# Sums in PSUM at a register's column, and one gathered tile in sixteen copied on chip: a graph network layer on one core

## The chip, the cores and the metric

The kernel runs on one core of a Trainium2 chip. The core's engines are TensorE (PE, with its weight loads as PEld), VectorE (DVE), ScalarE (ACT), GpSimd (POOL) and SyncE (SP, which here only starts DMAs). Each works through its own list of instructions in order; they meet at semaphores. The metric is the device time of one launch in microseconds (us), the median of several runs.

## The reference

A graph of 12,500 nodes with 64 features and 200,000 edges with 32. The edges come sorted by destination `dst`; the sources `src` are random. Cut to what matters:

```
def _mlp(x, W1, b1, W2, b2):
    return jax.nn.relu(x @ W1 + b1) @ W2 + b2
msg_in = jnp.concatenate([nodes[row], nodes[col], edge_features], axis=-1)   # row = src, col = dst
messages = _mlp(msg_in, mW1, mb1, mW2, mb2)                                  # 160 -> 128 -> 64
aggregated = jax.ops.segment_sum(messages, col, num_segments=nodes.shape[0])
upd_in = jnp.concatenate([nodes, aggregated], axis=-1)
update = _mlp(upd_in, uW1, ub1, uW2, ub2)                                    # 128 -> 128 -> 64
out = _layernorm(x + update)
```

Destinations follow 12500 times the square of a uniform number, so that in the sorted list the first edges share few nodes and the last ones are spread over many.

## The kernel before

**Tiling.** 128 edges are a tile (1563 tiles, the last partly padding), 8 tiles a group `s` (SUB, 196 groups), 16 tiles a super-group `g` (SUP, 98). The first layer of the message network is split: `A = x @ mW1[:64]` for the sources, `B = x @ mW1[64:128] + mb1` for the destinations, and the edge's own part. Both tables are made in the kernel in chunks of 1024 nodes (`chunk_a`, `chunk_b`, L381 to L403) and written to DRAM.

**Sources.** `gather` (L147) starts one indirect DMA on GpSimd per tile (L158): 128 rows of the table, by the source numbers in `src_s`, into a row buffer `xg` of one group (ROWB = 6 buffers). While A is not ready, the first XG = 7 groups fetch rows of x instead (64 wide, two groups to a buffer) and TensorE transposes and multiplies them (`transpose`, L257).

**Destinations.** As the edges are sorted, the destinations of a tile lie within a window of 32 nodes from the tile's first one, `wint`. `windows` (L206) reads these window starts into registers of SyncE and copies 32 rows of B per tile into `rhs`, beside the edge weights. `select` (L176, VectorE) makes two one-hot selections, one inside `operand` (with the edge features, so that one matmul gives edge part plus B row) and one in `sel`; `counts` (L194, ScalarE) makes a bf16 copy of the latter.

**A step.** The main loop (L537) handles one group a step. `edge_part` (L243, TensorE, for the next group) puts the edge part and the B row into PSUM `pc`; `node_part` adds the gathered row (L263, VectorE) and applies the relu (L264, ScalarE); `collect` multiplies each tile's hidden layer by its selection (L276, 8 matmuls into `ph`, 32 columns each) and one matmul with `one0` gives the counts (L274); `aggregate` (L279, VectorE) loads the 8 window starts into registers and adds each tile's 32 columns of sums and counts into `comb` in SBUF at the column of its window (L288, 8 adds that follow one another).

**Node updates.** `comb` holds for all nodes the 128 summed hidden features, the counts, a row of ones and x transposed. An update handles 384 nodes (UB = 3 tiles). There are 54; `UPD` lists at which super-group each begins, every 2 to 15 super-groups in the first 62 and every single one from there. Each is spread over steps: `columns` (a copy of the x part, ScalarE, L297), `update` (L304, L305 on TensorE, relu on ScalarE), `residual` (L315, L316 and the statistics), `norm` (reciprocal, scaling, store by SyncE).

**What sets the order.** The order in each engine's list is the order of the program (a manual schedule); buffers that rotate make a later writer wait for the last reader. PSUM: `pc` two buffers of two banks, and one bank each for `pt`, `ph`, `pu` and `cps`. A fallback for inputs that break the window rule follows behind a flag and does not run here.

## Time and profile before

| | |
|---|---|
| median of 10 runs | 1990.76 us (1989.14 to 1994.73) |
| the profiled execution | 1991.83 us, its span 1990.0 us |
| busy, share of the span | PE 68%, PEld 60%, DVE 46%, ACT 18%, POOL 74% |
| granted TensorE clock, mean | 0.576 of full speed |
| DMA | 211.74 MB, 106 GB/s on the mean |
| instructions | DVE 2661, ACT 479, PE 7851, POOL 1572 |

The page cuts the span into 40 slices:

```
PE   3678976656566566666666666757767758577687
DVE  5347643534343444444444444445454545454544
POOL 7677777777777777777777777777777777777773
PEclk9965555555555555555556555565565665655655
```

A digit is the busy share in tenths (for PEclk the clock that the throttle granted). In the lists of groups, a line gives source line, engine, operation, output<-inputs and shapes, the number of instructions, then after the bar the busy time in us, the mean of one in ns, the idle time just before them and what ended it ("issue": the engine waited for nothing that the profile shows). A q behind an engine's name (DVEq, SPq) is its queue: register operations, waits and DMA starts, which are not counted as busy; their rows give shortest, median and longest in ns. TensorE's fp32 matmuls have two rows each.

### The profile page before, as it was taken

To read this page: it belongs to the slowest core of one execution; us is meant where nothing else is said; L and a number is where in the kernel's file an instruction comes from. 1 tells how busy PE (TensorE), PEld (TensorE's weight loads), DVE (VectorE), ACT (ScalarE), POOL (GpSimd) and SP (SyncE) were. 2 spreads that over 40 slices of the span, in tenths; PEclk is the share of its full clock that TensorE was granted. 3 is DMA by queue.
4 is the path that set the end of the run, shared out by engine and by line. 5 is a ranking of instruction groups with operands and counts; after the bars stand their busy time and mean duration, and the time that the engine had idled before them with its cause. 6 is when DMAs were issued, how large, how long until landed. Compare 5 with 4: busy or idle time off the path is not lost.

```text
span 1990.0 us, 31593 instructions
## 1 busy us (share of the span) xinstructions
PE 1351.1 (68%) x7851; PEld 1198.9 (60%) x7851; DVE 908.4 (46%) x2661; ACT 348.3 (18%) x479; POOL 1476.5 (74%) x1572
## 2 busy tenths in 40 slices
PE   3678976656566566666666666757767758577687
PEld 3577865656555565665655655647666647475666
DVE  5347643534343444444444444445454545454544
ACT  1121111111111111111111111121212112121211
POOL 7677777777777777777777777777777777777773
PEclk9965555555555555555556555565565665655655
DMA  8745554433333333333333333333333333333331
GB/s 219 219 118 151 159 139 117 115 88 100 87 100 89 100 90 100 91 91 98 99 91 99 92 100 91 98 96 97 98 96 100 97 99 97 100 95 101 95 99 43
DMA packets 244401, 211.74 MB, mean 106 GB/s; under 512 B 80542, under 2 KB 209022, under 8 KB 243824
## 3 DMA queue, kind: packets, MB, share of 16 engines
q0 software_dynamic: 50016, 100.70, 19.9%
q1 hardware_dynamic: 178644, 98.69, 17.9%
q10 hardware_dynamic: 15554, 10.31, 1.8%
q8 instruction: 63, 1.03, 0.2%
q14 instruction: 124, 1.02, 0.2%
HBM read 190.78 MB, written 18.68 MB: 105 GB/s over the span
## 4 chain that ended last, share of the span: by engine, by line
POOL 54%; issue 25%; DMA 8%; PE 8%; DVE 3%; SPq 1%; ACT 0%; ACTq 0%; DVEq 0%; POOLq 0%
POOL xg L158 54%; DMA xg<-tab_a,src_s 5%; PE ph L276 3%; DMA xl<-in_x1T 2%; PE pc L243 2%; DVE comb L288 1%; PE pu L304 1%; PE pb L381 1%; PE py L315 1%; DVE h L263 1%; PE pu L305 1%; PE py L316 0%; DMA rhs<-tab_b 0%; PE ph L274 0%; SPq L216 0%
## 5 line engine op out<-in xcount | busy, mean ns | idle before, releaser
L158 POOL DMA_INDIRECT xg<-tab_a,src_s x1507 | 1422.4, 944 | 468.7 <-issue 443.3
L276 PEld LDWEIGHTS ph<-sel,h 128*128 128x128 f32 x3126 | 601.6, 295 | 35.0 <-issue 35.0
L276 PE MATMUL ph<-sel,h 128*128 128x32 f32 x3126 | 593.1, 360 | 0.0
L263 DVE TENSOR_TENSOR h<-pc,xg 128x1024 f32<-128x1024 f32 (+1 forms) x190 | 230.8, 1215 | 774.9 <-DMA xg<-tab_a,src_s 712.8
L243 PE MATMUL pc<-rhs,l 64*128 64x128 f32 x3126 | 407.8, 413 | 69.7 <-DMA l<-in_eT 36.0
L288 DVE TENSOR_TENSOR comb<-comb,ph 128x64 f32 x1563 | 345.6, 221 | 201.8 <-ACT xw L297 82.0
L243 PEld LDWEIGHTS pc<-rhs,l 64*128 64x128 f32 x3126 | 352.8, 302 | 89.0 <-DVE rs L330 35.0
L264 ACT ACTIVATE h<-h 128x1024 f32<-128x1024 f32 (+1 forms) x190 | 199.2, 1049 | 919.2 <-DVE h L263 877.4
L304 PE MATMUL pu<-comb,w2u 128*128 x108 | 88.9, 927 | 260.6 <-DVE comb L288 260.6
L274 PE MATMUL ph<-selb,one 128*128 128x256 bf16 x196 | 74.4, 380 | 241.9 <-DVE comb L288 156.2
L304 PEld LDWEIGHTS pu<-comb,w2u 128*128 128x128 f32 x108 | 27.1, 311 | 276.0 <-DVE comb L288 276.0
L274 PEld LDWEIGHTS <-one 128*128 128x128 bf16 x196 | 26.6, 136 | 274.1 <-DVE comb L288 254.8
L185 DVE TENSOR_TENSOR l<-l,cps 128x1024 f32<-128x1024 int32 (+1 forms) x101 | 123.3, 1221 | 4.0 <-DMA rhs<-tab_b 0.5
L197 ACT CAST selb<-sel 128x512 bf16<-128x512 f32 x98 | 60.4, 616 | 326.3 <-DVE sel L189 298.9
L315 PE MATMUL py<-ux,xw 128*128 128x64 f32 x324 | 84.5, 353 | 0.7 <-ACT hTu L307 0.7
L316 PE MATMUL py<-u,hTu 128*128 128x64 f32 x324 | 81.7, 344 | 0.0
L305 PE MATMUL pu<-xw,uz 128*128 128x384 f32 x108 | 80.3, 847 | 0.0
L307 ACT ACTIVATE hTu<-pu,ub_s 128x384 f32<-128x384 f32 x54 | 31.4, 582 | 271.4 <-PE pu L305 271.4
L315 PEld LDWEIGHTS py<-ux,xw 128*128 128x128 f32 x324 | 66.6, 255 | 10.7 <-issue 5.6
L316 PEld LDWEIGHTS py<-u,hTu 128*128 128x128 f32 x324 | 67.9, 259 | 0.0
L189 DVE TENSOR_TENSOR sel<-cps,drc 128x512 f32<-128x512 f32 x98 | 66.9, 682 | 0.1
L158 POOL DMA_INDIRECT xg<-in_x,src_s x56 | 53.0, 947 | 18.7 <-issue 16.2
(73 smaller groups left out, 419.1 us busy)
## 6 DMA issues: line engine op xcount, KB each, us to landing
l<-in_dst_row SPq DMA_DIRECT2D x196, 128.0 KB
l<-in_eT SPq DMA_DIRECT2D x196, 128.0 KB
rhs<-tab_b SPq DMA_DIRECT2D x1563, 16.0 KB
xg<-tab_a,src_s POOLq DMA_INDIRECT x1507
tab_b<-tb SPq DMA_DIRECT2D x13, 512.0 KB
tab_a<-tb ACTq DMA_DIRECT2D x12, 512.0 KB
out<-o SPq DMA_DIRECT2D x54, 96.0 KB
comb<-in_x1T SPq DMA_DIRECT2D x6, 520.0 KB
```

Of the source, the lines that this page charges most:

```text
L158: nc.gpsimd.indirect_dma_start(out=a[:, i, :], out_offset=None, in_=A[:, :] if s >= XG else x[:, :], in_offset=bass.IndirectOffsetOnAxis(a ...
L185: nc.vector.tensor_tensor(l[r], l[r].bitcast(I32), node[r].unsqueeze(2).broadcast_to([r.stop - r.start, SUP // 2, P]), op=ALU.is_equal)
L243: nc.tensor.matmul(pc[:, b, k, :], L[g][q:q + 64, m, :], rhs[g % 2][q:q + 64, m, :], start=s >= XG or k == 0, stop=s >= XG)
L263: nc.vector.tensor_tensor(h[:, b, m], pc[:, b, m], a[:, b, m], op=ALU.add)
L264: nc.scalar.activation(h[:, b, m], h[:, b, m], AF.Relu)
L274: nc.tensor.matmul(ph[:, :n, 1, :], one0, SB[g][:, k0:k0 + n, :], start=True, stop=True)
L276: nc.tensor.matmul(ph[:, i, 0, :], h[:, i % 2, i // 2, :], S[g][:, k0 + i, :], start=True, stop=True)
L288: nc.vector.tensor_tensor(to, to, ph[:, i], op=ALU.add)
L304: nc.tensor.matmul(pu, w2u, comb[:, 0, bass.ds(n0, UB * P)], start=True, stop=False)
L305: nc.tensor.matmul(pu, uz, xw, start=False, stop=True)
L315: nc.tensor.matmul(py[:, i], xw[:, i * P:(i + 1) * P], ux, start=True, stop=False)
L316: nc.tensor.matmul(py[:, i], hT[:, i * P:(i + 1) * P], u2, start=False, stop=True)
```

## The change

1. *Sums and counts add up in PSUM.* `aggregate` and `comb` go. The whole period of an update, up to 384 columns, has one PSUM bank for sums (`sums`, two buffers) and one for counts (`cnt`). `opened` starts them with a matmul of zeros; `collect` loads 8 column offsets (`woff`, worked out once by `offsets`) into registers of TensorE and each tile's matmul adds at its offset; counts are 8 matmuls with a single column of ones. `carry` adds the 32 columns of the last window to the next period; `close` copies the banks to SBUF (ScalarE). The x columns of an update come by DMA (`columns`), no longer from `comb`. `pu`, `py` and the set-up matmuls share the rotation of `pc`.
2. *One tile of each two groups is not gathered.* From group 13 on, the last tile of each odd full group (`copied`) gets its x columns, 64x1 each, from `xcol` (x transposed, in SBUF): 128 copies at a column from a register, spread over two steps, 36 of each 64 on ScalarE and 28 on VectorE (`copies`), into one of two `xo`. A further matmul with `w1a` in `edge_part` makes its row of A, and its relu reads PSUM alone.
3. *Row buffers and order.* ROWB 6 to 14, XG 7 to 8; the row buffer has the order of `pc`. `windows` is called for a group, two steps ahead, instead of for a super-group. `relative`, `windows` and the offsets stand later among the first chunks; the memsets of `comb` are gone. The store of a finished update moves to the end of its step.

```
-ROWB = 6
-XG = 7
+ROWB = 14
+XG = 8
+CG = 2
+CF = 6 * CG
+CA = 36
+UW = UB * P
+    def copied(s):
+        return s >= CF and s % CG == CG - 1 and len(tiles(s)) == SUB
...
-        for i, t in enumerate(tiles(s)):
+        for i, t in enumerate(tiles(s)[:SUB - copied(s)]):
             nc.gpsimd.indirect_dma_start(
...
+                c = copied(s) and i == n - 1
                 nc.tensor.matmul(pc[:, b, k, :], L[g][q:q + 64, m, :], rhs[g % 2][q:q + 64, m, :],
-                                 start=s >= XG or k == 0, stop=s >= XG)
+                                 start=s >= XG or k == 0, stop=s >= XG and not c)
+                if c:
+                    nc.tensor.matmul(pc[:, b, k, :], xo[s // CG % 2][q:q + 64], w1a[q:q + 64], start=False, stop=True)
...
-                    nc.scalar.activation(h[:, b, m], h[:, b, m], AF.Relu)
+                    nc.scalar.activation(hf[:, m], hf[:, m], AF.Relu)
+                if copied(s):
+                    nc.scalar.activation(h[:, 1, SUB // 2 - 1], pc[:, 1, SUB // 2 - 1], AF.Relu)
...
+        def opened(u):
+            ps = psum.tile([DH, UW], F32, name="sums")
+            pn = psum.tile([1, UW], F32, name="cnt", bufs=1)
+            nc.tensor.matmul(ps, zero_b[:, :P], zero_b, start=True, stop=False)
+            sums[u] = ps, pn
...
-            nc.tensor.matmul(ph[:, :n, 1, :], one0, SB[g][:, k0:k0 + n, :], start=True, stop=True)
+            _, ws = nc.values_load_multi_w_load_instructions(
+                woff[0:1, s * SUB:s * SUB + n], engines=[ET.PE], min_val=0, max_val=UW - WIN,
+                skip_runtime_bounds_check_because="they are limited to this")
             for i in range(n):
-                nc.tensor.matmul(ph[:, i, 0, :], h[:, i % 2, i // 2, :], S[g][:, k0 + i, :], start=True, stop=True)
+                nc.tensor.matmul(ps[:, bass.ds(ws[i], WIN)], h[:, i % 2, i // 2, :], S[g][:, k0 + i, :],
+                                 start=False, stop=ends and i == n - 1)
+            if s == 0 or period[s - 1] != u:
+                nc.tensor.matmul(pn, zero_b[:, 0:1], zero_b, start=True, stop=False)
             for i in range(n):
-                to = comb[:, :, bass.ds(ws[i], WIN)]
-                nc.vector.tensor_tensor(to, to, ph[:, i], op=ALU.add)
+                nc.tensor.matmul(pn[:, bass.ds(ws[i], WIN)], one, SB[g][:, k0 + i, :], start=False,
+                                 stop=ends and i == n - 1)
+        def carry(u):
+            d = nc.values_load(ustep[0:1, u:u + 1], engines=[ET.PE], ...)
+            nc.tensor.matmul(ps[:, :WIN], ident, sums_s[(u - 1) % 2][:, bass.ds(d, WIN)], start=False, stop=False)
+            nc.tensor.matmul(pn[:, :WIN], ident[:, 0:1], xw[(u - 1) % 2][:, bass.ds(d, WIN)], start=False, stop=False)
+        def close(u):
+            nc.scalar.copy(sums_s[u % 2], ps)
+            nc.scalar.copy(xw[u % 2][0:1], pn)
+        def copies(s):
+            t = (s + 2) // CG * CG + CG - 1
...
+            def by_dve(o, i):
+                nc.vector.tensor_tensor(o, i, slot[D:, 0:1], op=ALU.add)
+            for a, b, e, copy in ((k, k + CA // 2, ET.Activation, nc.scalar.copy),
+                                  (k + CA // 2, k + CA, ET.Activation, nc.scalar.copy),
+                                  (k + CA, k + n, ET.DVE, by_dve)):
+                _, v = nc.values_load_multi_w_load_instructions(srow[r:r + 1, a:b], engines=[e], ...)
+                parts += [(copy, a + i, v[i]) for i in range(b - a)]
+            for copy, i, v in parts:
+                copy(to[D:, i:i + 1], xcol[D:, bass.ds(v, 1)])
...
-            nc.scalar.copy(xw, comb[:, 1, bass.ds(n0, UB * P)])
+            nc.sync.dma_start(xw[u % 2][ONE:], x1T[:, bass.ds(n0, UW)])
...
-            if j == 0 and g + 1 < NSUP:
-                windows(g + 1)
+            if s + 2 < NSUB:
+                windows(s + 2)
             if s < NSUB:
                 node_part(s)
-            if s in due and s < last:
-                columns(due[s])
             if 1 <= s <= NSUB:
                 collect(s - 1)
-                aggregate(s - 1)
...
+            copies(s)
             if s + 1 < NSUB:
...
                 edge_part(s + 1)
-            if s == NSUB:
-                columns(K - 1)
+            if s in due and due[s] + 1 < K:
+                carry(due[s] + 1)
             if s in due:
-                update(due[s], "pt" if s == last else "pu")
+                update(due[s])
             if s - 1 in due:
-                residual(due[s - 1], "pt" if s - 1 == last else "pu")
+                residual(due[s - 1])
+            if s + 1 in due:
+                close(due[s + 1])
+            if s + 2 in due:
+                columns(due[s + 2])
             rest(s)
+            if s - 2 in due:
+                store(due[s - 2])
```

## The prediction

> **What bounds the kernel now.** I read the chain that ended last, then the costliest group, then that group's timeline. Words used: a *step* handles one group s of 8 tiles; a *pair* is two steps, g = s/2; a *late* pair is one of the last 36 (g from 62), where every pair has a node update. Both page lines:

> ```profile
> POOL 54%; issue 25%; DMA 8%; PE 8%; DVE 3%; SPq 1%; ACT 0%; ACTq 0%; DVEq 0%; POOLq 0%
> L158 POOL DMA_INDIRECT xg<-tab_a,src_s x1507 | 1422.4, 944 | 468.7 <-issue 443.3
> ```

> GpSimd's indirect gathers and the 0.30 us between them are 79% of the chain. Of their 468.7 us of idle time 443.3 is that issue gap and nearly nothing is a wait for a buffer. The timeline of GpSimd:

> ```profile
> 82.99 0.94 POOL L158 DMA_INDIRECT xg<-tab_a,src_s  x1 [9.55 <-DMA rhs<-tab_b]
> ...
> 1001.11 0.94 POOL L158 DMA_INDIRECT xg<-tab_a,src_s  x1 [0.30 <-issue]
> ...
> 1029.84 0.94 POOL L158 DMA_INDIRECT xg<-tab_a,src_s  x1 [0.30 <-issue]
> ```

> Rows 1001.11 and 1029.84 are 23 gathers apart: 1.249 us each. The only large gap is 9.55 us at 83, before the first gather from the table A. So the time is 1563 gathers x 1.249 = 1952, plus 2.8 ahead of them, about 10 of gaps and 25.5 us behind the last one (it ends at 1964.5): 1990. A step of 8 gathers lasts 9.99 us, and the other engines have idle time in it. The question is how much the change puts there.

> **What it removes.** `copied` is true for groups 13, 15 ... 193: 91 gathers less, 91 x 1.249 = 113.7 us. A copying pair then lasts 15 x 1.249 = 18.74 instead of 19.99.

> **What it moves at the start.** Eight groups instead of seven are gathered from x, so the first gather from A comes due at 83.6 instead of 73.4, and the 9.55 us wait goes if A is still ready by 83. But the load of `relative`, now after chunk 4, takes one of the two `tb` buffers in mid-stream. Before, the extra `tb` user after chunk 0 cost the next chunk's copy 11.4 us of waiting. Bounds: the whole 9.55 gained, or 2 lost. I take 5.3 gained. The eight memsets of `comb` (2.75 us each, VectorE) held one matmul burst; I count nothing for them. The 14 row buffers cost nothing and gain nothing while gathers do not wait for buffers; they let GpSimd run ahead when others lag.

> **What it adds: the column copies.** Per step 36 on ScalarE and 28 on VectorE, each a register operation and a copy of 64x1, after register loads of 18+18 and 28. The trace has the queue parts, in the answers by line:

> ```profile
> L283 DVEq TENSOR_LOAD <-wint x196: 593/597/853, 76.9 to 1971.5; - x196
> ...
> L288 DVEq FUSED_REGOPS  x1563: 69/69/69, 77.8 to 1976.4; - x196
> ...
> L297 ACTq FUSED_REGOPS  x54: 46/46/52, 338.9 to 1975.1; - x54
> ```

> A load of 8 registers takes 0.60; one takes 0.28 (L294) and sixteen 0.97 (L211), so 0.046 per further register. Estimate: 18 take 1.06, two such 2.13; 28 take 1.53. No row shows the copy. Its bounds come from these timeline rows:

> ```profile
> 1003.75 1.23 DVE L263 TENSOR_TENSOR h<-pc,xg 128x1024 f32<-128x1024 f32 x1 [5.21 <-DMA xg<-tab_a,src_s]
> 1004.89 2.00 DVE L288 TENSOR_TENSOR comb<-comb,ph 128x64 f32 x8
> 1006.81 0.22 DVE L183 TENSOR_SCALAR cps<-wh,pidx 128x8 f32<-128x8 int32 x1
> ...
> 1009.20 0.30 DVE L322 BATCH_NORM_AGGREGATE mv<-st 128x2 f32<-128x6 f32 x3
> ...
> 1968.08 0.62 ACT L264 ACTIVATE h<-h 128x256 f32<-128x256 f32 x2 [1.54 <-DVE h L263]
> ```

> VectorE low: three tiny instructions in 0.30 at 157 ns each start 72 ns apart. High: eight L288 in 2.00 start 255 apart, each with a register operation and a wait for the one before. The copies have no such wait. In the queue's records a register operation holds VectorE's queue for 119 ns and an instruction's dispatch some 48: I take b = 167. ScalarE: L264 takes 416 ns at 256 columns and 1056 at 1024, so 203 fixed; its two rows start 323 apart, so 93 overlap: low a = 110. High: 203 with no overlap behind a register operation that holds the queue 85 ns: 288. I take a = 85 + 45 = 130, since nothing waits between the copies.

> [...]

> Sums, against 18.74. ScalarE, normal pair: 2 x 2.13 + 72a = 4.26 + 9.36 = 13.6. VectorE, normal: add 1.14, select 1.99 (1006.81 to 1008.80), two loads 3.06, 56b = 9.35: 15.5. Both fit. In a late pair the engines wait for each other: ScalarE's square root `sd` now stands behind 36 copies, and VectorE's reciprocal, scaling (1.0) and the odd step's add stand behind it. VectorE then: add and select 3.13, ScalarE's loads 2.13, 36a = 4.68, sqrt 0.4, norm 1.0, load 1.6 (the add is under it), 28b = 4.68: 17.6, 1.1 to spare. ScalarE, select to select: 6.8 + 72a = 16.2. The cover is thin: from b = 0.21 alone, or a = 0.16 alone, the late pairs run over.

> **What it adds on TensorE, removes on VectorE.** The 1563 adds of L288 (8 in 2.00 us per step) go. TensorE sums at a register's column: 16 register operations of 37 ns and a load of 0.6 per step, in the queue ahead of the array. Counts become 8 one-column matmuls per step instead of one L274. Their price lies between 26 ns (L507's spacing) and 250 (an L276 pass of 213 and the register operation); I take 100, near L507, as one column is loaded.

> ```profile
> 190.10 3.46 PE L276 MATMUL ph<-sel,h 128*128 128x32 f32 x16
> 193.49 2.08 PE L243 MATMUL pc<-rhs,l 64*128 64x128 f32 x16
> ...
> 165.40:254.00 88.60, 78.46 (x475) 73.31 (x476) 56.80 (x152) 15.77 (x17) 66.96 (x72) 0.50 0.55 151
> 1300.00:1900.00 600.00, 427.08 (x2463) 364.60 (x2462) 287.71 (x930) 119.31 (x180) 453.34 (x482) 0.60 0.37 98
> ```

> At half clock a late pair takes: sums and edge matmuls 2 x 5.54 = 11.1, counts 1.6, loads 1.2, opening two banks 0.6 (384 bf16 columns each; L274's 256 hold the array 0.19, 189.91 to 190.10), carry 0.63, the x columns 0.21, update 2.56, residual 12 x 0.213 = 2.56: 20.5, over 18.74. At the granted 0.60 of 1300 to 1900 us, a fifth of the time runs at full clock, where an L276 pass is 112 instead of 213: 18.74 holds 18.74 x (0.8 + 0.2 x 1.9) = 22.1. It fits by 1.6, and a normal pair (14.1) easily.

> [...]

> SyncE: two window loads of 8 instead of one of 16 (+0.2), 54 loads of x columns (about 0.7 with their register): about 12.5 of 18.74; its copies land a step earlier than needed. Moved stores (`store` at the step's end) delay nothing that is read.

> Sum against the profiled execution: 1990.0 - 113.7 - 5.3 = 1871.0; the median stands 0.76 above that span: 1872.

> **Rivals.** (1) The late pairs slip, with VectorE behind ScalarE's square root, or TensorE without its fifth at full clock (20.5: +1.8 x 34 = 60). At b = 0.255: 20.1, +1.3 x 34 = 46; a = 0.16 more: +37. Time 1885 to 1950, about 1915. For: 1.1 us to spare on two unseen prices. Against: the row buffers spread what one pair is late.
> (2) Slower: ScalarE's copies become the bound in every copying pair. 57 normal pairs at 4.26 + 72a and 34 late ones at 6.8 + 72a, some 155 us before and 40 behind: equal to before at a = 0.20; at the upper bound 0.288 it is 25.0 and 27.5, so 155 + 1425 + 935 + 40 = about 2555. For: no row has a register-addressed copy back to back. Against: 85 + 45 in the queue and the overlap.
> (3) The gathers are saved and the start eats them (table A late by 2 and more, backlog of TensorE at half clock): 1880. It changes little; it is in the range.

> **How the numbers follow.** Forecast with (3) 0.62, rival (1) 0.20, rival (2) 0.17, something within 0.2% 0.01. Within 0.2%, about 4 us, is what these runs cannot tell from no change. The likeliest case alone: 1861 (no wait for A, a tail shorter by 5) to 1885. The range takes in (1): 1861 to 1950. Faster 0.82, same 0.01, slower 0.17.

> **What would show it.** 1472 gathers still 1.25 apart, with issue as the releaser to the end; the gap before the first gather from A under 10; copies about 0.13 apart on ScalarE and 0.17 on VectorE; late pairs of 18.7. Wrong if gathers wait for `h` or `xg`, if the copies are over 0.2 apart, or if TensorE has no gaps in the late pairs.

## The result and the profile after

| | before | after |
|---|---|---|
| median | 1990.68 us (30 runs) | 2124.80 us (9 runs, 2113.82 to 2126.05) |
| ratio after / before | | 1.0658, 95% interval 1.0646 to 1.0669 |
| profiled execution, its span | 1990.0 us | 2123.1 us |
| gathers, last one started | 1563, 1963.6 us | 1472, 1960.8 us |
| a normal pair / a late pair | 19.99 us (16 gathers x 1.249) | 20.58 / 21.89 us |

The pairs of the changed kernel are measured between the relus of the copied tiles (L290), one per pair: the mean of 44 spacings before the late pairs begin (those that end at pairs 17 to 60) and of 33 within them (63 to 95). Of the 44, the 29 without a node update last 19.62 and the 15 with one 22.43. 18.74 was forecast for both, the time 1872. The chain that ended last, by engine and by line:

```profile
issue 23%; POOL 23%; ACTq 23%; ACT 16%; PE 7%; DMA 4%; DVE 3%; DVEq 1%; SPq 0%; POOLq 0%
POOL xg L176 23%; ACTq L353 22%; ACT xo L358 11%; PE sums L315 2%; ACT h L288 2%; DMA xl<-in_x1T 2%; DVE h L287 1%; PE pc L264 1%; ACT selb L216 1%; PE pu L373 1%; DMA xg<-tab_a,src_s 1%; PE pu L374 1%; DMA tab_a<-tb 1%; DVE o L402 1%; ACT hTu L376 1%
```

More than half of GpSimd's share (54% before) has gone, and ScalarE has 39%, 23 of them in its queue: L353, the register loads of the copies. The costliest groups say where the idle time is:

```profile
L176 POOL DMA_INDIRECT xg<-tab_a,src_s x1408 | 1328.8, 944 | 549.6 <-issue 410.1
L358 ACT COPY xo<-xcol 64x1 f32 x6552 | 686.2, 188 | 806.9 <-issue 800.5
L347 DVE TENSOR_TENSOR xo<-xcol,cps 64x1 f32<-64x1 f32 x5096 | 665.0, 158 | 198.5 <-issue 198.5
```

ScalarE stood idle for 807 us ahead of its copies, "issue": it waited for no other engine. GpSimd's idle time is now 139 us more than its issue gap; before it was 25 us more. The answer for line 353 (shortest, median, longest of one load in ns):

```profile
L353 ACTq TENSOR_LOAD <-srow x364: 1452/3280/5194, 161.0 to 2069.8; - x182
L353 DVEq TENSOR_LOAD <-srow x182: 1847/1898/2166, 159.2 to 2066.5; - x182
```

1.06 us was forecast for a load of 18 on ScalarE, 1.53 for the load of 28 on VectorE. VectorE's 28 registers cost less than the median of ScalarE's 18. And ScalarE's median hides two kinds: taken one by one in the queue's records, the first load of each step has a median of 1.505 us and the second, of the same size, 3.954. A window of the chain, within late pairs (start us, us, what):

```profile
1501.04 0.95 ACT h L288
...
1502.63 3.87 ACTq L353
...
1510.69 0.58 ACT hTu L376
...
1512.72 3.42 ACTq L353
...
1520.34 0.30 ACT sd L393
1520.67 0.19 DVE rs L399
...
1521.73 1.01 DVE h L287
...
1522.99 0.94 POOL xg L176
```

This is the circle of a late pair: relu, loads, 36 copies, the update's relu, loads, 36 copies, square root `sd`, then VectorE's reciprocal, scaling and the odd step's add, which frees a row buffer for GpSimd and lets the next relu go. The list of waits (engine and line, what for, total us, times, longest) shows the two ends of it:

```profile
DVE rs L399 <- ACT sd L393: 225.8, 54, 6.2
...
POOL xg L176 <- DVE h L287: 127.7, 35, 6.6
```

The normal pairs were late as well (20.58), but the 14 buffers took it up until 1112 us; from there gathers wait.

### The profile page after: what moved, and what is told of

Same layout as the page of the kernel before. It is cut to its first block, busy times and chain, and to the rows that moved or that the text cites. A ratio compares the mean times of both kernels' runs of the same rounds, so it can differ in the third digit from the quotient of the medians.

```text
span 2123.1 us, 58914 instructions
## 1 busy us (share of the span) xinstructions
PE 1541.2 (73%) x9740; PEld 1346.7 (63%) x9740; DVE 1215.7 (57%) x6199; ACT 1046.4 (49%) x7177; POOL 1391.0 (66%) x1481
## 3 DMA queue, kind: packets, MB, share of 16 engines
q8 instruction: 92, 1.51, 0.3%
## 4 chain that ended last, share of the span: by engine, by line
issue 23%; POOL 23%; ACTq 23%; ACT 16%; PE 7%; DMA 4%; DVE 3%; DVEq 1%; SPq 0%; POOLq 0%
POOL xg L176 23%; ACTq L353 22%; ACT xo L358 11%; PE sums L315 2%; ACT h L288 2%; DMA xl<-in_x1T 2%; DVE h L287 1%; PE pc L264 1%; ACT selb L216 1%; PE pu L373 1%; DMA xg<-tab_a,src_s 1%; PE pu L374 1%; DMA tab_a<-tb 1%; DVE o L402 1%; ACT hTu L376 1%
## 5 line engine op out<-in xcount | busy, mean ns | idle before, releaser
L176 POOL DMA_INDIRECT xg<-tab_a,src_s x1408 | 1328.8, 944 | 549.6 <-issue 410.1
L358 ACT COPY xo<-xcol 64x1 f32 x6552 | 686.2, 188 | 806.9 <-issue 800.5
L347 DVE TENSOR_TENSOR xo<-xcol,cps 64x1 f32<-64x1 f32 x5096 | 665.0, 158 | 198.5 <-issue 198.5
L315 PEld LDWEIGHTS sums<-sel,h 128*128 128x128 f32 x3126 | 633.0, 304 | 126.2 <-ACT h L288 90.9
L315 PE MATMUL sums<-sel,h 128*128 128x32 f32 x3126 | 629.7, 373 | 71.2 <-ACT h L288 70.0
L264 PE MATMUL pc<-rhs,l 64*128 64x128 f32 x3126 | 384.8, 413 | 91.2 <-DVE o L402 77.8
L264 PEld LDWEIGHTS pc<-rhs,l 64*128 64x128 f32 x3126 | 331.3, 303 | 110.5 <-DVE o L402 79.9
L288 ACT ACTIVATE h<-h 128x1024 f32<-128x1024 f32 (+1 forms) x189 | 187.9, 995 | 103.6 <-DVE h L287 94.8
L320 PEld LDWEIGHTS <-one 128*1 128x1 bf16 x1563 | 64.8, 83 | 252.0 <-issue 237.0
L267 PE MATMUL pc<-w1a,xo 64*128 64x128 f32 x182 | 60.6, 430 | 113.5 <-ACT xo L358 110.7
L267 PEld LDWEIGHTS pc<-w1a,xo 64*128 64x128 f32 x182 | 42.7, 289 | 127.7 <-ACT xo L358 124.5
L320 PE MATMUL cnt<-selb,one 128*1 128x32 bf16 x1563 | 97.0, 188 | 0.3
L373 PE MATMUL pu<-sums_s,w2u 128*128 128x384 f32 x108 | 89.0, 928 | 1.5 <-ACT sums_s L334 1.5
```

Source lines behind the costliest of these rows:

```text
L176: nc.gpsimd.indirect_dma_start(out=a[:, i, :] if s < XG else a[:, i // 2, i % 2, :], out_offset=None, in_=A[:, :] if s >= XG else x[:, :], ...
L264: nc.tensor.matmul(pc[:, b, k, :], L[g][q:q + 64, m, :], rhs[g % 2][q:q + 64, m, :], start=s >= XG or k == 0, stop=s >= XG and not c)
L288: nc.scalar.activation(hf[:, m], hf[:, m], AF.Relu)
L315: nc.tensor.matmul(ps[:, bass.ds(ws[i], WIN)], h[:, i % 2, i // 2, :], S[g][:, k0 + i, :], start=False, stop=ends and i == n - 1)
L320: nc.tensor.matmul(pn[:, bass.ds(ws[i], WIN)], one, SB[g][:, k0 + i, :], start=False, stop=ends and i == n - 1)
L347: nc.vector.tensor_tensor(o, i, slot[D:, 0:1], op=ALU.add)
```

## The experiments

Theory A was that ScalarE's register loads alone made the pairs long, and the rest of the change does what the prediction says. Its rivals were TensorE (B) and the copies themselves (C).

**Without the copies.** `copied` returns False.

```
-        return s >= CF and s % CG == CG - 1 and len(tiles(s)) == SUB
+        return False
```

> No group is copied: all 1563 gathers are made, no register load and no column copy on ScalarE or VectorE; the sums and counts in PSUM, the new start and the 14 row buffers stay. Theory A (ScalarE's register loads, 5.4 us a step instead of 2.13, make the pairs too long; the rest of the change is within its time): GpSimd sets the pace again, 1563 x 1.249 + 2.8 + a gap of 4.6 before the first gather from A + 25 = 1985 us, no wait for a row buffer. Rival B (TensorE's sums and counts with a node update per pair need 21.7 us by themselves): the 36 late pairs stay at 21.7 against 19.99, about +61, so about 2045.

1987.45 us, ratio to before 0.9969 [0.9958, 0.9980]. All 1563 gathers run without a wait for a buffer; of GpSimd's waits, these are the issue gaps and the one ahead of the first gather from A:

```profile
POOL xg L176 <- issue: 447.5, 1467, 0.3
...
POOL xg L176 <- DMA tab_a<-tb: 1.2, 1, 1.2
```

So the sums and counts in PSUM, the windows per group and the new start cost nothing: they gain 0.31%, some 6 us. B falls for pairs of 19.99.

**Copies without register loads.**

```
-                _, v = nc.values_load_multi_w_load_instructions(srow[r:r + 1, a:b], ...)
-                parts += [(copy, a + i, v[i]) for i in range(b - a)]
+                parts += [(copy, i, i) for i in range(a, b)]
...
-                copy(to[D:, i:i + 1], xcol[D:, bass.ds(v, 1)])
+                copy(to[D:, i:i + 1], xcol[D:, v:v + 1])
```

> The copies are made, 36 and 28 a step, but from fixed columns, so the register loads (L353) and the register operations of the copies go; the x columns of the copied tiles are then the wrong ones. Theory A: the 8.1 us that ScalarE idles in a late pair before its first copies go, 21.8 - 8.1 = 13.7, under 18.74, and GpSimd sets the pace: 1865 to 1885 us. Rival B: late pairs stay near 21.7, 2040 to 2125. Rival C (the copies themselves are too long): late pairs between, 1900 to 2040.

1875.45 us, 0.9404 [0.9388, 0.9420]; normal pairs 18.71, late ones 18.80. B and C fall: TensorE and the copies fit under 18.74. What is left is the loads and register operations.

**Four forms of the load.** A pair in four each has ScalarE's 36 values as 18 and 18; 28 and 8; 18, copies, 18, copies; 9 four times.

```
+            load, sizes, between = [(load18, (18, 18), False), (load28and8, (28, 8), False),
+                                    (load18between, (18, 18), True), (load9, (9, 9, 9, 9), False)][r % 4]
+            a = k
+            for size in sizes:
+                v = load(ET.Activation, a, a + size)
...
```

> ScalarE's 36 values of a step come in four forms, by the pair: 18 and 18 as now; 28 and 8; 18, their 18 copies, then 18 and their copies; four times 9. VectorE's stay one load of 28. Theory A1 (a load is dear, 3.9 us, when another load stands directly before it): with the copies between, both loads take about 1.5; 28 and 8: 2.1 and about 3; four of 9: 0.7, then three near 3. Theory A2 (each register costs ScalarE about 0.15, paid by whichever load the first use waits for): every form sums to about 5.4, and with copies between each of the two takes 2.7. Theory A3 (the last load before a use carries 2.4 us, whatever its size): with copies between both take 3.9, sum 7.8; 28 and 8: 2.1 and 3.0; four of 9: 0.7, 0.7, 0.7, 3.1. The time itself is between 2050 and 2180 us in all.

2084.93 us (one run). The medians of each load, from the records of ScalarE's queue, with the byte of its row of `srow`, counted from the row's start, at which it begins (a step begins at 0 or at 256, which I leave out):

| form | loads: registers at byte, us |
|---|---|
| 18, 18 | 18 at 0: 1.52; 18 at 72: 3.97 |
| 28, 8 | 28 at 0: 1.78; 8 at 112: 0.56 |
| 18, copies, 18, copies | 18 at 0: 1.51; 18 at 72: 4.01 |
| 9, 9, 9, 9 | 9 at 0: 0.81; 9 at 36: 2.01; 9 at 72: 2.01; 9 at 108: 2.00 |

A1, A2 and A3 all fall: a load in second place can be cheap (8 at 112), and it stays dear with copies ahead of it. The order does not separate the cheap from the dear; the address does. 0 and 112 are multiples of 16 bytes, 36, 72 and 108 are not. Off a multiple, each register costs (3.97 - 2.01) / 9 = 0.22 us. On one, four cost (1.78 - 0.56) / 5 = 0.24. That was theory A4: one read per 16 bytes, or one per register. No record shows the reads themselves; A4 is a form that these prices fit.

**The address alone, two ways.** First ScalarE's loads become 20 and 16, at bytes 0 and 80:

```
-            for a, b, e, copy in ((k, k + CA // 2, ET.Activation, nc.scalar.copy),
-                                  (k + CA // 2, k + CA, ET.Activation, nc.scalar.copy),
+            for a, b, e, copy in ((k, k + 20, ET.Activation, nc.scalar.copy),
+                                  (k + 20, k + CA, ET.Activation, nc.scalar.copy),
```

> ScalarE's 36 values are loaded as 20 and 16 instead of 18 and 18, so both loads begin at a multiple of 16 bytes in srow (0 and 80, or 256 and 336; the second load of 18 begins at 72 or 328). Nothing else changes. Theory A4 (a load reads 16 bytes at a time where it begins at a multiple of 16 and one register at a time where it doesn't, about 0.213 us a read and 0.09 besides): 0.09 + 5 x 0.213 = 1.15 and 0.09 + 4 x 0.213 = 0.94, 2.1 a step instead of 5.4; the late pair on ScalarE is 21.8 - 2 x 3.3 = 15.2, under 18.74, GpSimd sets the pace, and the time is 1868 to 1890 us. Rival A3 (the last load before its use is dear whatever its address): loads 1.1 and 3.4 or more, late pairs 20.8 or more, 2060 or more.

Then the loads stay as in the changed kernel, and every value lies 8 bytes further on:

```
-    srow = const.tile([NCT, P], I32, name="srow")
+    srow = const.tile([NCT, P + 4], I32, name="srow")
...
-                    srow[r:r + 1, a:b], engines=[e], ...
+                    srow[r:r + 1, a + 2:b + 2], engines=[e], ...
...
-                nc.sync.dma_start(srow, src_row[...][:NCT])
+                nc.sync.dma_start(srow[:, 2:2 + P], src_row[...][:NCT])
```

> srow is two columns wider at its front and every load begins 8 bytes later; 18 and 18 on ScalarE and 28 on VectorE as in the changed kernel. Theory A4: ScalarE's first load now begins off a multiple of 16 (8 or 264) and its second on one (80 or 336), so the prices change places, about 3.9 first and 1.47 second; VectorE's load of 28 begins at 152 or 408, off it, and takes 0.09 + 28 x 0.213 = 6.05 instead of 1.9; the time is over 2150 us, with VectorE in the way too. Rival A5 (the second load of a step is dear because it is the second): 1.47 and 3.9 as before, VectorE 1.9, and the time 2125 us as before.

And the first with 6 row buffers (`ROWB = 6`):

> As e4_aligned, with 6 row buffers as in the kernel before instead of 14. If the prediction's step on the buffers holds (14 gain nothing while gathers do not wait for buffers), the time is that of e4_aligned within 0.3%. Rival: late pairs are each late by turns and the buffers take it up; then gathers wait for buffers and the time is 10 to 40 us above e4_aligned.

These three ran on a chip on which the kernel before took 2807 us, 41% more than elsewhere; their times, 2759.26, 2940.53 and 2718.44, say nothing of the question. The loads themselves do. Line 353 of the shifted kernel:

```profile
L353 ACTq TENSOR_LOAD <-srow x364: 1454/2704/5270, 348.5 to 2886.9; - x182
L353 DVEq TENSOR_LOAD <-srow x182: 6244/6447/7783, 348.7 to 2881.1; - x182
```

One by one, ScalarE's first load took 4.02 us and its second 1.49: they changed places. VectorE's 28 went from 1.90 to 6.45, its median. A5 falls, and with 20 and 16 the loads took 1.29 and 1.03.

The next three runs fell on such a chip again (before 2806.66 us): 2758.63, 2725.23 and 2924.56 us. On both chips the kernel with 6 buffers took less than that with 14, by 1.5 and 1.2%; on the others the two are the same, as shown below; why is open. The runs repeated two kernels and added one in which ScalarE copies 28 columns and VectorE 36:

```
-CA = 36
+CA = 28
...
+            for a, b, e, copy in ((k, k + CA, ET.Activation, nc.scalar.copy),
+                                  (k + CA, k + 48, ET.DVE, by_dve),
+                                  (k + 48, k + n, ET.DVE, by_dve)):
```

> The same kernel as e4_aligned, once more: the kernel before took 2807 us on the chip of that run against 1990 on others, so its time told nothing. Loads of 1.3 and 1.0 us are already seen there. Theory A4: 2.3 a step instead of 5.4, the late pair on ScalarE 21.8 - 6.2 = 15.6, under 18.74, GpSimd sets the pace: 1868 to 1890 us. Rival B2 (PE, at 90% of the time in e2_no_loads, is so near its end that anything more of waiting makes the late pairs long): 1890 to 1960, with gathers waiting for buffers late in the span.

> The same kernel as e6_aligned_rows6, once more: e4_aligned with 6 row buffers instead of 14. The prediction's step: within 0.3% of e4b_aligned. Rival: pairs are late by turns and the buffers take it up, so with 6 the gathers wait and it is 10 to 40 us above.

> ScalarE copies 28 columns a step (one load, begun at a multiple of 16 bytes, about 1.75 us) and VectorE 36 (loads of 20 and 16 at offsets 112 and 192 bytes, 2.3 us together). ScalarE's late pair falls by some 2 x (0.5 + 8 x 0.103) = 2.6 and VectorE's grows by 2 x (0.4 + 8 x 0.130) = 2.9: VectorE would be at 3.13 + 1.0 + 0.8 + 2 x (2.3 + 4.7) = 18.9, its waits not counted. If VectorE is as near its end as this sum says, the late pairs pass 18.74 and the time is 10 to 60 us above e4b_aligned; if the loads and copies lie beside other work, it is the same within 0.3%.

**The same on chips like the first.** Loads of 20 and 16:

> The kernel of e4_aligned a third time: the kernel before took 2807 us in the runs of the first two, against 1990 to 1995 in the others. Theory A4 (ScalarE's loads at a multiple of 16 bytes cost 2.3 us a step instead of 5.4, the late pair on ScalarE is about 15.6, GpSimd sets the pace): 1868 to 1890 us. Rival B2 (PE, at 90% of the time in e2_no_loads, is so near its end that the loads' remaining 2.3 us a step make the late pairs long): 1890 to 1960, with gathers waiting for buffers late in the span.

1870.42 us (1869.99 to 1872.34), 0.9401 [0.9388, 0.9414]: 6.0% under before, where the changed kernel is 6.6% over it, with one split moved by two columns. Its line 353, its costliest group, its window of late pairs (busy PE, PEld, DVE, ACT, POOL, then the granted clock, DMA share, GB/s), and ScalarE's timeline in a late pair:

```profile
L353 ACTq TENSOR_LOAD <-srow x364: 998/1164/1483, 157.6 to 1815.4; - x182
L353 DVEq TENSOR_LOAD <-srow x182: 1847/1899/2223, 155.7 to 1812.3; - x182
```

```profile
L176 POOL DMA_INDIRECT xg<-tab_a,src_s x1408 | 1328.6, 944 | 429.2 <-issue 403.9
```

```profile
1205.00:1800.00 595.00, 542.89 (x3296) 468.45 (x3293) 424.35 (x2269) 378.41 (x2544) 449.74 (x477) 0.56 0.40 108
```

```profile
1511.88 0.30 ACT L393 ACTIVATE sd<-mv,eps 128x3 f32<-128x3 f32 x1
...
1514.36 0.95 ACT L288 ACTIVATE h<-h 128x896 f32<-128x896 f32 x1 [1.46 <-DVE h L287]
1515.21 0.26 ACT L290 ACTIVATE h<-pc 128x128 f32<-128x128 f32 x1
1516.97 3.72 ACT L358 COPY xo<-xcol 64x1 f32 x36 [1.50 <-issue]
```

In the changed kernel the row of the copies at the same place was

```profile
1506.67 1.10 ACT L358 COPY xo<-xcol 64x1 f32 x10 [4.52 <-issue]
```

ScalarE idles 1.50 us between relu and copies instead of 4.52. Gathers never wait for a buffer, and the late pairs last 18.76. TensorE is busy 542.89 of 595 us, 91%, at a clock of 0.56: by this figure a limit is near, but no run has a pair short enough to show it.

With 6 row buffers, and with 28 columns on ScalarE:

> e4c_aligned (1870.4 us) with 6 row buffers instead of 14. The prediction's step, that 14 buffers gain nothing while gathers do not wait for buffers: 1865 to 1876. Rival: pairs are late by turns and the buffers take it up, so with 6 the gathers wait: 1880 to 1910.

> e4c_aligned with 28 columns a step on ScalarE (one aligned load) and 36 on VectorE (aligned loads of 20 and 16). By the prediction's sum for VectorE with measured prices, 3.13 + 1.0 + 0.8 + 2 x (2.3 + 4.7) = 18.9 in a late pair without its waits, against 18.74: if that sum decides, late pairs pass 18.74 and the time is 1880 to 1930. If loads and copies lie beside other work, 1866 to 1876.

6 buffers: 1872.86 us, 0.9401 [0.9389, 0.9414], the same. 28 on ScalarE: 1901.77 us, 0.9543 [0.9516, 0.9570], late pairs of 19.58. VectorE's timeline there:

```profile
1506.58 4.69 DVE L347 TENSOR_TENSOR xo<-xcol,cps 64x1 f32<-64x1 f32 x36 [1.60 <-issue]
...
1512.50 0.17 DVE L399 RECIPROCAL rs<-sd 128x3 f32<-128x3 f32 x1 [0.36 <-ACT sd L393]
```

VectorE waits 0.36 us for ScalarE and otherwise hardly for anybody but its own loads (1.38 and 1.13 us). The expectation's sum with these prices is 3.13 + 1.0 + 0.8 + 2 x (2.51 + 4.69) = 19.3, against 19.58. TensorE is no rival here: it is busy 538 of 595 us, from 1205 to 1800, much as with 36 columns on ScalarE (543), and from 1205 to 1840 us no wait of VectorE for TensorE is listed. The buffers cover what the gathers would have waited, and it is paid behind the last gather: 57.9 us from its start to the end instead of 28.0.

## Why the prediction was wrong

The step that failed is one term: "18 take 1.06, two such 2.13". Two loads took 1.505 + 3.954 = 5.46 us a step. The slope of 0.046 per register came from loads of 1, 8 and 16 in the kernel before. All loads of 8 and 16 there begin at a multiple of 16 bytes, since their offsets are multiples of 8 registers; the row could not show what a load at byte 72 costs, and I gave the load no bounds at all while I bounded the copy twice. Four times 0.046, 0.18, is near the 0.24 that four registers cost at a multiple of 16 bytes; off one, a single register costs 0.22. With that one term put right, by the split alone, gathers set the pace again and the time was 1870.42.

The other steps, against the runs:

- *Gathers saved, 113.7 us.* Right. (Of the chain before, the gathers and the gaps between them are 77% and not 79: 34 us of its issue lie on other engines.) The two ratios 0.9969 and 0.9401 of the 1990.68 us are 1984.5 and 1871.4 us, 113.1 apart, between the kernel without copies and that with loads of 20 and 16.
- *Start, 5.3 us gained.* Right within what can be told: 6 us for all that is not copies (4 to 8 by the interval). Ahead of the first gather from A, GpSimd idled 3.6 us in the changed kernel and 0.3 to 4.2 in its variants on chips like that one, against 9.55.
- *Copies.* Cheaper than taken: 36 in 3.72 us on ScalarE, 0.103 each (130 ns taken, 110 the low end), and 28 in 3.65 on VectorE, 0.130 each (167 taken, 72 to 255 the bounds). One ScalarE copy lasts 188 ns, but the next starts 101 ns after it, before its end, as in the row L264 (two of 416 and 293 ns, 323 apart).
- *ScalarE's pairs.* With the measured prices the prediction's own late sum gives 16.2 - 4.26 - 9.36 + 2 x 5.46 + 72 x 0.103 = 20.9, and 21.89 was seen. That sum left out the relus, the cast of the counts and the update's relu (0.95 + 0.26 + 1.05 + 0.61 + 0.58 = 3.45 us), but part of the loads lies under them: ScalarE idled 4.52 + 3.58 us ahead of its copies for loads of 10.9. Its normal sum left out the relus and the cast too (1.06 + 0.95 + 0.26 + 0.60): 10.9 + 7.4 + 2.9 = 21.2, against 19.62 in the pairs without an update, again with part of a load under the relus. With cheap loads the omissions cost nothing.
- *TensorE, 20.5 at half clock.* It fitted, in the kernel with loads of 20 and 16 at the clock named above, 0.56 instead of the 0.60 that I took from before (0.59 there from 1500 to 1700 us, with TensorE busy 89%). No run tested it under a shorter pair. The half clock is that of the stretch from 165 to 254 us in the kernel before. TensorE idled 4.56 us in it up to 170.98 and 2.68 up to 231.82; but from 171 to 202 us it had no gap of 0.1 us, and the granted clock stayed 0.50, so the reading holds.
- *VectorE, 1.1 us to spare.* Shown: 8 more columns a step on it, and the late pairs pass 18.74 (19.58). (The normal sum counts one of the two adds of a pair; with the other, 1.1 us, it is 16.6, still under 18.74.)
- *14 buffers gain nothing while gathers do not wait.* Shown with loads of 20 and 16 (1872.86 us with 6, 1870.42 with 14). In the changed kernel and with 28 on ScalarE, where pairs are too long, the end lies 162 and 58 us behind the last gather's start, against 28; fewer were not tried there.
- *Rivals.* It went the way of rival (2), ScalarE bound in every copying pair, with the load in place of the copy. Its sum with the measured pairs is 57 x 20.58 + 34 x 21.89 + 155 + 40 = 2112, against a span of 2123. I made it depend on the copy's price alone, and gave it 0.17.

The forecast of 1872 us is what the change does (1870.42) once ScalarE's second load begins at byte 80 instead of 72. That it agrees to 2 us is in part luck: the wait for A was 0.3 us in that run, 4 less than the forecast took, and 4.2 in the run with 6 buffers.

## What to carry to other kernels

The price of a register load from SBUF depended here on the address at which it begins. So begin each at a multiple of 16 bytes (18 registers took 1.5 us on one and 4.0 off it) and make its size a multiple of four registers (20 took 1.29 us, less than 18): 36 registers cost 2.3 us as 20 and 16, and 5.5 us as 18 and 18. When a price comes from a row of the same operation, ask in what the new use differs from all uses in that row, the address included, and give that difference a bound. When idle time ends with "issue", look at the engine's queue records one by one, since a median over two kinds shows neither.
